# One block for the whole body, ordered on the scheduler's timeline machine, and the rest of the queries written in place

## The chip, the cores and the metric

The kernel runs on one NeuronCore of a Trainium2 chip. The metric is the device time of one execution in microseconds. Five engines work side by side, each with a queue of its own that it takes in order: TensorE (PE, with its weight loads shown apart as PEld), VectorE (DVE), ScalarE (ACT), GpSimd (POOL) and SyncE (SP), which here issues every DMA.

## What is computed

A two-layer gated cross-attention network in the manner of Flamingo, on x of 4 x 512 x 512 and a context of the same size, all float32. Four residual steps follow each other:

```python
x = x + tanh(g_xattn[0]) * wkv(w, u, layernorm(x), ctx)          # a recurrence over the 512 tokens
x = x + tanh(g_ffn[0]) * bit_ffn(layernorm(x), w1, w2, w3)       # D 512, hidden 2048, 1-bit weights
x = x + tanh(g_xattn[1]) * int8_attention(layernorm(x), ctx)     # 16 heads of 32
x = x + tanh(g_ffn[1]) * ternary_linear(rms(layernorm(x)), W)    # D 512
```

- wkv keeps a running weighted mean per channel: `p, q, o` are the numerator, the denominator and the running maximum, and the output is `(A*p + E*v) / (A*q + E)`.
- bit_ffn is `(silu(Q(x) @ B1.T) * (Q(x) @ B2.T))` quantised once more and multiplied by `B3.T`. Q rounds groups of 64 channels to 8 bits, B is the sign of the weight times its mean magnitude.
- int8_attention rounds the normalised x and wq, wp to 8 bits by rows; keys and values come from the context in full precision; scores, softmax and output projection follow.
- ternary_linear rounds the rows to 8 bits and the weights to -1, 0, 1.

## The kernel before

The four batches of 512 tokens go through the same four steps. P is 128, so a batch has NT = 4 row tiles of 128 tokens, and D has NC = 4 column blocks. Until about 90 us the first batch's recurrence, the context's keys and values and the first weights are made; then the feed-forward layer of one batch runs with other work aside of it.

**Steps and places.** Each layer is a Python generator that traces a few instructions and yields. `line` (L1222) gives a generator a place on a common scale, and `run` (L1206) always advances the one whose place is lowest. The trace order is so written by hand: feed-forward of batch b (64 steps from b to b + 16/17), the recurrence of the next batch aside of it (L1334 to L1342), the attention of the batch before (L1359), and the ternary layer of the one before that (L1371).

**The order on the engines.** The trace order isn't yet the order on the chip. The tile framework's scheduler plays the traced program on a model of the chip. When an engine of the model is free, it is given, of the traced instructions whose inputs are there and whose buffer is free, the earliest traced. The order in which this happens is the order of that engine's queue in the program; buffers are given out in that order too. The model used by default is one of two that the framework has; the other one is called the timeline machine. Two means of the kernel bind the scheduler: `behind` (L135) adds an edge without a wait that keeps one instruction after another on the same engine, and `in_turn`, `next_turn` (L147, L156) use it to keep every matmul and transpose behind the last one of the turn before. `tc.keep_in_program_order` (L193) pins the statistics of the recurrent layer.

**The recurrence** (`wkv_layer`, L562) runs on chunks of 128 channels. For each of the four chunks of a batch, DVE runs three scans over 512 tokens (L599, L629, L634) and a reciprocal in two halves (L640), POOL six products and sums (L608 to L642), ACT the exponentials (L612, L614).

**The feed-forward** (`ffn_layer`, L702) has 16 units per batch, a row tile and a quarter of the hidden size each. For a unit PE multiplies twice into a PSUM bank `ff_hp` (L733); ACT L745 takes the tanh of the first, DVE L746 reads the same bank, DVE L750 multiplies the second in; `quantised` (L671) rounds the result on DVE, ACT (L684) and POOL (L685), `parts` (L690) transposes it and splits it in two for `ff_acc` (L764). The weights `wT` are loaded again for each batch by SP (L724) into a ring of five buffers.

**The attention** (`attention_layer`, L840) has 16 units per batch, a pair of heads and half of the rows each. `scores` (L937) multiplies (`s_ps`), DVE L948 takes the maxima, ACT L950 the exponentials; `turned` transposes (`pt_ps`), ACT L970 or DVE L968 copies; `values` multiplies (`o_ps`). Before them `project` (L887) makes the queries of a group of four heads. It writes the scaled queries `q` (DVE L898), their rounded half `half[0]` (ACT L903) and the rest `half[1]` (DVE L904), and stores both halves to DRAM (SP L908), from where `fetch_queries` loads them rearranged (L913).

**Row buffers.** `row` (L856) takes a buffer of 128 x 512 float32 under the tag `at_row`, of which there are ROWS = 3. `at_q`, `at_half`, the normalised rows `at_xn` (POOL L219), the projected output `at_y` and the ternary layer's `tf_xn` all take theirs from these three. A buffer is free again when everything that reads it has ended, a DMA when it has landed.

Of the kernel before, what the change touches and what calls it, by code (L numbers as in the profile page):

```python
# [11 lines left out]
F32R = mybir.dt.float32r  # L12
# [18 lines left out]
def kernel(  # L31
# [34 lines left out]


    nc = tc.nc
    NB, T, D = x.shape
    FF = w1.shape[0]  # L70
    NT, NC, NF = T // P, D // P, FF // D
# [59 lines left out]
    def bank(name, dtype=F32):  # L131

        return psum_tile(name, "m", dtype)
# [27 lines left out]
    def matmul(*args, **kwargs):  # L161
        return in_turn(nc.tensor.matmul(*args, **kwargs))  # L162
# [677 lines left out]
    def attention_layer(b, xb, pool, tiles=range(NT)):  # L840
# [5 lines left out]
        lo, n = tiles[0] * P, len(tiles) * P  # L846
# [9 lines left out]
        def row(name, dtype=F32):  # L856
            return pool.tile([P, D], dtype, name=name, tag="at_row", bufs=ROWS)
# [29 lines left out]
        def project(g):  # L887
            qp = bank("q_ps")[:, 0:n]
            for c in range(NC):
                matmul(  # L890
                    qp,
                    lhsT=wqT[:, c, g * P : (g + 1) * P],
                    rhs=xqT[:, c, lo : lo + n],
                    start=(c == 0),
                    stop=(c == NC - 1),
                )
            q = row("at_q")[:, 0:n]
            nc.vector.scalar_tensor_tensor(  # L898
                q, qp, sq[:, g : g + 1], sxb[:, lo : lo + n], ALU.mult, ALU.mult
            )  # L900
            half = [row("at_half", F32R)[:, 0:n] for _ in range(2)]
            bias = bqc[:, g : g + 1]
            nc.scalar.activation(half[0], q, AF.Identity, bias=bias)  # L903
            nc.vector.scalar_tensor_tensor(  # L904
                half[1], q, bias, half[0].bitcast(F32), ALU.add, ALU.subtract
            )
            for i in range(2):
                nc.sync.dma_start(out=qD[b][g][i, :, lo : lo + n], in_=half[i].bitcast(F32))  # L908
# [83 lines left out]
        def collect(k):  # L992
# [14 lines left out]
            )  # L1007

        project(0)
        fetch_keys(0)  # L1010
        fetch_values(0)
        fetch_queries(0)
        yield
        project(1)
        fetch_queries(1)
        yield
# [45 lines left out]
        for k in range(len(units) + 2):  # L1062
# [29 lines left out]
            if now:  # L1092
                p, h = units[k]
                if h == 0:
                    if p + 1 < NP:
                        fetch_keys(p + 1)
                    if p % 2 == 0 and p // 2 + 2 < NC:
                        next_turn()
                        project(p // 2 + 2)
                elif p % 2 and p // 2 + 1 < NC:  # L1100
                    fetch_values(p // 2 + 1)
                if k + 2 < len(units):
                    fetch_queries(k + 2)
# [320 lines left out]
```

## Time and profile before

| | |
|---|---|
| median of 3 runs | 1096.12 us (1095.92 to 1096.5) |
| the profiled execution, its own time | 1094.21 us |
| its span, first to last instruction | 1092.4 us |
| granted TensorE clock, mean | 0.956 |
| instructions | 17928 |
| HBM read, written | 148.65 MB, 39.85 MB |

Over the span, in 40 equal slices, the busy tenths (9 is 90% or more), the granted PE clock and the share of the DMA engines:

```profile
## 2 busy tenths in 40 slices
PE   3879997998879888799997886999999999878975
...
DVE  5985548757876899896769898966687866579976
ACT  5656755567545776667877576677685777877863
POOL 3831104423333254621215545412122410100000
PEclk8889999999999999999999798999999999989998
DMA  8188845464445674645576354655574563244311
```

A slice is 27.3 us. The first three hold the start, the next eight the first batch's feed-forward with weights being made; from about slice 13 to 25 the recurrence of the next batch, attention and feed-forward run together; the last six are the last batch's attention and ternary layer without feed-forward. "Idle before" in the groups and the timeline is the time an engine stood before an instruction, and the name behind the arrow is the instruction or DMA whose end released it.

### The profile page before, as it was taken

The numbers are of one execution on the slowest core, as the hardware profiler recorded it, in microseconds if no ns is written. First come the engines' busy times: TensorE is split into PE (matmuls) and PEld (weight loads), VectorE is DVE, ScalarE is ACT, GpSimd is POOL, SyncE is SP. The second block draws the span as 40 slices with busy tenths as digits, with TensorE's granted clock in tenths as the row PEclk, the third lists the DMA queues.
The fourth block names the chain that finished last, engine by engine and source line by source line (L and its number), as shares of the span: only waits on it lengthen the run. The fifth ranks groups of instructions, "written<-read, shape, count | busy, mean of one in ns | idle before, by whom it ended". The sixth has DMA issues, their size and how long they took to land.

```text
span 1092.4 us, 17928 instructions
## 1 busy us (share of the span) xinstructions
PE 943.3 (86%) x6350; PEld 680.0 (62%) x6380; DVE 827.0 (76%) x1600; ACT 729.9 (67%) x1490; POOL 320.7 (29%) x328
## 2 busy tenths in 40 slices
PE   3879997998879888799997886999999999878975
PEld 2345564565557666677775665677776777655652
DVE  5985548757876899896769898966687866579976
ACT  5656755567545776667877576677685777877863
POOL 3831104423333254621215545412122410100000
PEclk8889999999999999999999798999999999989998
DMA  8188845464445674645576354655574563244311
GB/s 288 39 272 317 323 169 190 144 221 155 154 146 181 221 234 127 231 129 169 185 234 204 121 177 133 204 195 180 184 231 156 184 210 116 59 148 116 116 42 39
DMA packets 85674, 189.68 MB, mean 174 GB/s; under 512 B 12241, under 2 KB 36817, under 8 KB 74577
## 3 DMA queue, kind: packets, MB, share of 16 engines
q1 hardware_dynamic: 85584, 188.53, 51.7%
q8 instruction: 51, 0.84, 0.3%
q14 instruction: 39, 0.31, 0.1%
HBM read 148.65 MB, written 39.85 MB: 173 GB/s over the span
## 4 chain that ended last, share of the span: by engine, by line
PE 49%; DVE 22%; ACT 14%; POOL 5%; issue 5%; DMA 4%; SPq 1%; ACTq 0%; POOLq 0%; DVEq 0%
PE ff_hp L162 15%; PE pt_ps L165 7%; PE ff_acc L162 6%; PE o_ps L162 4%; PE v_ps L162 4%; PE s_ps L162 3%; ACT at_P L950 3%; DVE wk_q L640 3%; ACT at_PT L970 3%; DVE at_nm L948 2%; PE k_ps L162 2%; DVE wk_p L634 1%; PE qr_ps L165 1%; PE tp_ps L165 1%; ACT wk_e L612 1%
## 5 line engine op out<-in xcount | busy, mean ns | idle before, releaser
L162 PE MATMUL ff_hp<-wT,xp 128*128 128x512 f32 x1024 | 275.7, 412 | 6.6 <-DVE ff_z L746 3.7
L162 PEld LDWEIGHTS ff_hp<-wT,xp 128*128 128x128 f32 x1024 | 195.4, 196 | 54.6 <-DVE ff_z L746 5.7
L950 ACT ACTIVATE at_P<-s_ps,at_nm 128x512 f32<-128x512 f32 x256 | 175.0, 690 | 45.2 <-DVE at_nm L948 43.4
L948 DVE TENSOR_REDUCE at_nm<-s_ps 128x1 f32<-128x512 f32 x256 | 166.6, 677 | 38.4 <-PE s_ps L162 37.9
L970 ACT COPY at_PT<-pt_ps 128x512 f32<-128x512 f32 x224 | 131.2, 590 | 72.6 <-PE pt_ps L165 71.9
L685 POOL TENSOR_TENSOR ff_z<-qg_b,qg_s 128x512 f32<-128x512 bf16 x64 | 71.9, 1124 | 314.6 <-ACT qg_b L684 304.7
L165 PE MATMUL pt_ps<-ident,at_P 128*128 128x128 f32 x1024 | 155.4, 280 | 9.0 <-ACT at_PT L970 4.3
L165 PEld LDWEIGHTS pt_ps<-ident,at_P 128*128 128x128 f32 x1024 | 118.1, 142 | 47.3 <-ACT at_PT L970 10.9
L162 PE MATMUL ff_acc<-wT,hr 128*128 128x512 f32 x512 | 137.6, 409 | 5.2 <-DVE hr L697 2.6
L162 PE MATMUL s_ps<-at_kR,at_qR 128*128 128x512 f32 x256 | 103.0, 464 | 24.0 <-ACT at_P L950 17.6
L162 PEld LDWEIGHTS ff_acc<-wT,hr 128*128 128x128 f32 x512 | 92.9, 191 | 26.2 <-DVE hr L697 4.2
L162 PE MATMUL o_ps<-at_PT,at_V 128*32 128x128 f32 x2048 | 75.4, 281 | 4.7 <-ACT at_PT L970 2.8
L162 PEld LDWEIGHTS o_ps<-at_PT,at_V 128*32 128x32 f32 x2048 | 54.8, 111 | 28.6 <-issue 11.6
L746 DVE SCALAR_TENSOR_TENSOR ff_z<-ff_z,ff_hp 128x512 f32<-128x512 f32 x64 | 43.4, 679 | 37.0 <-ACT ff_z L745 36.9
L745 ACT ACTIVATE ff_z<-ff_hp,coef 128x512 f32<-128x512 f32 x64 | 44.1, 688 | 40.5 <-PE ff_hp L162 38.1
L750 DVE SCALAR_TENSOR_TENSOR ff_z<-ff_hp,coef,ff_z 128x512 f32<-128x512 f32 x64 | 47.7, 745 | 30.2 <-PE ff_hp L162 30.1
L684 ACT CAST qg_b<-qg_i 128x512 bf16<-128x512 int8 x80 | 49.3, 617 | 27.4 <-DVE qg_i L680 17.3
L162 PEld LDWEIGHTS s_ps<-at_kR,at_qR 128*128 128x128 f32 x256 | 43.3, 194 | 36.4 <-ACT at_P L950 25.2
L162 PE MATMUL v_ps<-wkvT,cT 128*128 128x512 f32 x128 | 60.5, 618 | 5.5 <-DVE wT L303 2.3
L162 PE MATMUL k_ps<-cT,wkvT 128*128 128x512 f32 x128 | 61.3, 631 | 2.3 <-ACT wk_k L584 1.0
L640 DVE RECIPROCAL wk_q<-wk_q 128x256 f32<-128x256 f32 x32 | 54.5, 1722 | 3.0 <-POOL wk_q L635 1.6
L696 ACT CAST hr<-tp_ps 128x512 fp32r<-128x512 f32 x64 | 37.6, 588 | 21.7 <-PE tp_ps L165 21.7
(180 smaller groups left out, 1669.4 us busy)
## 6 DMA issues: line engine op xcount, KB each, us to landing
wT<-wD SPq DMA_DIRECT2D x72, 1024.0 KB, 5.4
wn<-in_L_ffn_w_dram SPq DMA_DIRECT2D x18, 1024.0 KB, 6.2
at_kR<-kD SPq DMA_DIRECT2D x128, 128.0 KB, 4.0
at_qR<-qD SPq DMA_DIRECT2D x256, 64.0 KB, 2.5
wD<-wT SPq DMA_DIRECT2D x12, 1024.0 KB, 4.2
kD<-k_half SPq DMA_DIRECT2D x16, 512.0 KB, 2.8
qD<-at_half SPq DMA_DIRECT2D x32, 256.0 KB, 2.2
cn<-in_ctx_dram SPq DMA_DIRECT2D x8, 512.0 KB, 5.9
```

The lines of the kernel that those rows point to most:

```text
L162: return in_turn(nc.tensor.matmul(*args, **kwargs))
L165: return in_turn(nc.tensor.transpose(*args))
L640: nc.vector.reciprocal(half, half)
L684: nc.scalar.copy(qb, qi)
L685: nc.gpsimd.tensor_tensor(grouped(src), grouped(qb), s.unsqueeze(2).to_broadcast([P, NG, GS]), ALU.mult)
L696: nc.scalar.copy(part[:, 0, :], pt)
L745: nc.scalar.activation(z, hp, AF.Tanh, scale=coef[:, 0:1])
L746: nc.vector.scalar_tensor_tensor(z, z, 1.0, hp, ALU.add, ALU.mult)
L750: nc.vector.scalar_tensor_tensor(z, hp, coef[:, 1:2], z, ALU.mult, ALU.mult)
L948: nc.vector.tensor_reduce(nm, sp, AX.X, ALU.max, negate=True)
L950: nc.scalar.activation(lanes[k, i, t], sp, AF.Exp, bias=nm, accum_out=sums[k][:, t, i : i + 1],)
L970: made[k] = nc.scalar.copy(dst, blocks(pt))
```

## The change

Two edits. The first opens a block at the start of the body, which is closed when the body ends, so that every pool, tile and instruction of the body lies in it. The block is scheduled on the timeline machine in place of the default one. The edges of `behind` and the pin of L193 are kept. The second makes `half[1]`, the rest of the queries, no buffer of its own but the buffer of `q`, read as fp32r: L904 reads `q` and writes its result over it, and SP's second store of L908 reads it from there. A projection so takes two of the three row buffers.

```diff
     nc = tc.nc
+    ctx.enter_context(tc.block(schedule_with_timeline_sim=True))
     NB, T, D = x.shape
...
             nc.vector.scalar_tensor_tensor(
                 q, qp, sq[:, g : g + 1], sxb[:, lo : lo + n], ALU.mult, ALU.mult
             )
-            half = [row("at_half", F32R)[:, 0:n] for _ in range(2)]
+            half = [row("at_half", F32R)[:, 0:n], q.bitcast(F32R)]
             bias = bqc[:, g : g + 1]
             nc.scalar.activation(half[0], q, AF.Identity, bias=bias)
             nc.vector.scalar_tensor_tensor(
                 half[1], q, bias, half[0].bitcast(F32), ALU.add, ALU.subtract
             )
```

## The prediction

> **What bounds the kernel now.** I read the busy shares first, then the chain that ended last, then the stretches of the span, then the places where TensorE (PE) stood longest.
>
> ```profile
> PE 943.3 (86%) x6350; PEld 680.0 (62%) x6380; DVE 827.0 (76%) x1600; ACT 729.9 (67%) x1490; POOL 320.7 (29%) x328
> ...
> PE 49%; DVE 22%; ACT 14%; POOL 5%; issue 5%; DMA 4%; SPq 1%; ACTq 0%; POOLq 0%; DVEq 0%
> ```
>
> PE is the longest lane, but the chain runs through it for only 49%; VectorE (DVE) holds 22% and ScalarE (ACT) 14%. PE is idle 1092.4 - 943.3 = 149.1 us, and only that time and the boundaries of the program can move: the change takes no matmul away. The stretches say where it lies.
>
> ```profile
> 91.00:318.00 227.00, 201.59 (x908) 129.57 (x907) 150.84 (x256) 133.48 (x215) 58.38 (x60) 0.99 0.55 200
> ...
> 360.00:660.00 300.00, 260.14 (x1853) 200.49 (x1859) 257.06 (x465) 210.75 (x442) 118.37 (x117) 0.95 0.55 180
> ...
> 700.00:900.00 200.00, 192.74 (x1459) 149.69 (x1470) 146.84 (x335) 142.69 (x314) 48.28 (x48) 0.99 0.59 193
> ```
>
> After the bounds and the length come busy PE, PEld, DVE, ACT and POOL. From 700 to 900 us, where no recurrent layer runs aside, PE is idle 7.3 of 200. From 360 to 660, where the recurrent (WKV) layer of the next batch runs aside on DVE and POOL, it is idle 39.9 of 300, and DVE is busy 257.1 of 300. So where PE stands, the DVE queue is nearly full, and what counts is which of its instructions comes first. One such place:
>
> ```profile
> 458.35 0.68 ACT L745 ACTIVATE ff_z<-ff_hp,coef 128x512 f32<-128x512 f32 x1
> ...
> 459.62 2.18 POOL L635 TENSOR_TENSOR wk_q<-wk_q,wk_e 128x512 f32<-128x512 f32 x1
> ...
> 461.83 1.75 DVE L640 RECIPROCAL wk_q<-wk_q 128x256 f32<-128x256 f32 x1 [1.04 <-POOL wk_q L635]
> ...
> 463.50 0.63 DVE L746 SCALAR_TENSOR_TENSOR ff_z<-ff_z,ff_hp 128x512 f32<-128x512 f32 x1
> ...
> 464.18 2.15 PE L162 MATMUL ff_hp<-wT,xp 128*128 128x512 f32 x6 [3.67 <-DVE ff_z L746]
> ```
>
> L746 frees the PSUM bank for which the next matmuls wait. Its input is ready at 459.03, but it is queued behind L640 of the aside layer, which first waits 1.04 us for POOL and then runs 1.75; PE stands 3.67 us. The largest gap of the middle is of the same kind:
>
> ```profile
> 657.09 1.21 DVE L599 TENSOR_TENSOR_SCAN wk_o<-wc,wk_k 128x512 f32<-128x512 f32 x1
> 658.22 0.67 DVE L680 TENSOR_TENSOR qg_i<-ff_z,qg_r 128x512 int8<-128x512 f32 x1
> ...
> 658.80 0.15 DVE L1152 RECIPROCAL tf_s<-tf_s 128x1 f32<-128x1 f32 x1
> ...
> 661.05 1.11 PE L165 MATMUL qr_ps<-ident,tf_xn 128*128 128x128 f32 x4 [8.60 <-ACT tf_xn L231]
> ```
>
> A pair of reciprocals (3.37 us from 649.82) and then this scan run between the short steps on which ACT L231, and so PE, waits. From 91 to 1055 us PE has nine gaps of 2 us or more, together 32.9 us. Four follow a long DVE instruction of the aside layer: 4.13 (at 250.4), 3.67 (464.2), 2.70 (615.7), 8.60 (661.0), sum 19.1, mean 4.8. The other five sum to 13.8: 2.10, 2.21, 3.87, 2.22, 3.37.
>
> **The change, part by part.** *The other ordering machine.* It removes and adds no instruction of the computation; it may move any of the 1600 on DVE, 1490 on ACT, 328 on POOL and 621 DMA issues on SP. PE moves least: the edges of L137 to L150 hold each turn's matmuls behind the turn before, and the new block keeps them. So PE work stays at 943.3, and the price is what PE waits for. In the aside layers of batches 1 to 3, the recurrent layer has 12 chunks, each with three scans (L599, L629, L634, from 1.16 us) and two reciprocals (1.72): 60 long DVE instructions, each of which may land before something PE waits for. Today 4 of 60 do. The trace doesn't show the new order. Bounds: all nine gaps gone, -32.9; or one hit in each of the 12 chunks, 8 more at 4.8, +38.4. Between ends so far apart I go by the row it is nearest to, the stretch 360 to 660: DVE is 86% busy, so an instruction put in the wrong place finds no slack, and only 4 of 60 hits are left to be undone while 56 may be added. I take twice today's hits, +19.1, and half of the other five gaps dissolved by the reshuffle, -6.9: +12.2.
>
> The long ones also stretch each other:
>
> ```profile
> L635 POOL TENSOR_TENSOR wk_q<-wk_q,wk_e x16: 1264/1274/2192, 26.8 to 681.4; 128x512 f32<-128x512 f32 x16
> ...
> L634 DVE TENSOR_TENSOR_SCAN wk_p<-wk_e x16: 1210/1986/2293, 34.4 to 683.6; 128x512 f32<-128x512 f32 x16
> ```
>
> The columns are shortest, median and longest ns. The same shape takes 1.21 us or 2.29, so up to 1.08 us more where the two engines meet; an order that lets them meet more often pays this, and it is inside the 4.8 of a hit. The Trainium skill, page "SBUF — State Buffer", section "SBUF: two separate sides", says more: GpSimd and a DVE instruction with two SBUF inputs take one port pair in turn, and the later one is fully blocked. By that rule a meeting could cost a scan the whole 1.27 us of a POOL instruction instead of 1.08, and four new hits would cost 4 x 0.19 = 0.8 us more, an estimate of 1109 instead of the figure below; the rows show no scan that long, so the sum goes by the rows.
>
> *The block itself.* All engines enter and leave it once. No row shows such a boundary; it can't gain, as the same instructions stand before and behind. Nearest: 0.29 us of POOL idle behind its own sequencer at 0.71 us, and, as upper end, all that lies around the span, 1094.21 - 1092.4 = 1.8 us. I take the row of POOL doubled for entry and exit, +0.6.
>
> *The rest of queries over the scaled queries.* L904 still runs, 16 times at 752 ns, and writes over its own input. Each projection takes two row buffers of three instead of three. It adds a wait too: the buffer of q, before free when L904 ends, is now free when its DMA (L908) has landed, 2.2 us in the median, 4.1 at most. Queued behind that wait are the next projection's L898 on DVE, or POOL's L219 for the next normalised rows; for both, the third buffer is now free. The rows show the present wait once: ACT L903 idles 1.9 us at 361.85 for the landing of qD<-at_half, in the first layer. The tightest place is the last layer, 953 to 962 us, where no feed-forward covers: PE's gap of 3.37 at 961.64 ends with the load at_qR of the first projection, whose q, half and L908 come no earlier with the edit. So I take 0, with -1.9 (that wait gone) and +2.2 (one landing exposed) as ends. In the other three layers feed-forward matmuls (8 x 412 ns = 3.3 us a step) cover either; without them each layer would pay up to 2.2.
>
> *Sum.* +12.2 + 0.6 + 0 = +12.8 on the profiled execution, 1094.2 to 1107.0. The median of the runs is 1096.12, 1.9 above the profiled one, so I forecast 1096.1 + 12.8 = 1108.9, said as **1108**.
>
> **The rivals.** *A better order, so faster.* If the new order puts L746, L750, L948 and the short scale steps before scans and reciprocals, three of the four hits go: 3 x 4.8 = -14.3, and a quarter of the 27 gaps between 0.7 and 2 us from 91 to 700 (26.8 us), -6.7; with the block +0.6: 1096.1 - 20.4 = 1076. Two of the four hits alone: 1087. Middle: 1081. For it: 700 to 900 us shows that 3.6% idle is possible with the same feed-forward and attention, against 75.8 us idle (12.4% of 609) from 91 to 700. Against it: POOL's stretched 2.18 us at 459.62, for which L640 waited, would have to be foreseen, and DVE has little slack. It decides from the point where the hits fall below two.
>
> *SP becomes the late one.* SP issues every load and store and waits in order.
>
> ```profile
> SPq L724 <- PE ff_hp L162: 149.1, 27, 17.7
> ...
> SPq L1173 <- DVE xb L1172: 70.7, 11, 41.9
> ```
>
> L1173 stores outputs, L724 loads feed-forward weights, 1 MB each, 5.4 us to landing. If four of the weight loads come behind a store or a query store that waits (70.7 / 11 = 6.4 us each), and the five-deep ring doesn't cover them, PE waits about 4 x 6.4 = 25.7 more: with the forecast's sum 1134. For it: 16 stores and 32 query stores stand among 72 loads. Against it: today PE waits on DMAs only 4.2 us.
>
> *It does nothing on the path.* The edges hold PE, the aside work shifts within slack, and 1096.5 stays. Against it: 827 of 1092 us of DVE work may be reordered.
>
> **How the numbers follow.** Forecast (1098.5 to 1122) 0.41; SP late (above 1122) 0.17; better order (below 1094) 0.36; nothing 0.06. About 0.2% (2.2 us) is what a measurement of this kernel can tell from no change. The range leaves out one in ten on either side: 1074, a little under the better order's full price, to 1132, just short of SP's. As both signs hold most of the chance, the forecast's own range is 1099 to 1122, from half a hit more (+2.4) to a little over five (+26). Faster 0.36, same 0.06, slower 0.58.
>
> **What would show it.** Right: PE busy stays within 5 us of 943 while its idle time grows, in the stretches with the recurrent layer aside; eight or so gaps of 2 us or more end with a DVE or ACT instruction queued behind L599, L629, L634 or L640; the stretch with feed-forward and attention alone stays near 3.6% idle. Wrong: fewer such gaps and a DVE order that takes L746 before L640 (better order); PE gaps ended by wT or at_qR landings, with longer SP waits at L724 (SP late); a gap of some us at the first or last instruction (a dearer block); L898 or L219 waiting for a landing of at_half (a dearer in-place write).

## The result, and the profile after

| | before | after |
|---|---|---|
| median of the runs | 1096.02 us (1094.16 to 1096.5) | 1155.85 us (1153.67 to 1158.3) |
| ratio, 95% interval | | 1.0553 (1.0539 to 1.0567) |
| profiled execution, its span | 1092.4 us | 1151.8 us |
| granted TensorE clock, mean | 0.956 | 0.943 |
| PE idle, span less busy | 149.1 us | 194.3 us |

The change costs 60 us, five times what was forecast. Two executions further down ran far longer than the others of their kernel, at 2290 us (`block_default`) and 3972 us (`pin_dve`): they are counted in the medians and left out of the ratios. In the changed kernel every line number below the first edit is one higher (L163 is the matmul that was L162); the kernels further down add lines of their own. The busy line of the page after, and the shares of its chain of waits:

```profile
PE 957.5 (83%) x6350; PEld 689.5 (60%) x6380; DVE 831.6 (72%) x1600; ACT 730.0 (63%) x1490; POOL 320.6 (28%) x328
...
PE 48%; DVE 24%; ACT 15%; DMA 5%; issue 4%; POOL 4%; SPq 1%; ACTq 0%; DVEq 0%; POOLq 0%
```

The instructions of these engines are the same in number; ACT works as long as before, DVE 4.6 us longer. PE is idle 45.2 us longer and, with the same matmuls, busy 14.2 us longer. To see where, I cut both spans at the same instructions: the 1st, 257th, 769th and last of the 1024 `ff_hp` matmuls, which are the start of the first batch's feed-forward, of the second's, of the fourth's, and the end of it. The four stretches of the kernel after (columns as in the prediction: bounds, length, busy PE, PEld, DVE, ACT, POOL, clock, DMA share, GB/s):

```profile
0.00:109.10 109.10, 68.36 (x233) 38.04 (x233) 71.85 (x88) 67.50 (x121) 46.04 (x54) 0.84 0.68 234
109.10:364.80 255.70, 213.52 (x910) 136.06 (x910) 156.08 (x271) 128.60 (x207) 64.01 (x69) 0.92 0.47 161
364.80:790.90 426.10, 363.10 (x2523) 281.34 (x2534) 341.98 (x645) 284.50 (x595) 157.12 (x154) 0.96 0.53 175
790.90:977.40 186.50, 173.40 (x1315) 136.06 (x1324) 127.31 (x287) 125.92 (x275) 43.74 (x43) 1.00 0.54 177
```

and the second of them before:

```profile
100.20:328.60 228.40, 200.00 (x911) 130.47 (x910) 154.51 (x272) 134.12 (x215) 65.95 (x68) 0.99 0.54 192
```

Before, the four took 100.2, 228.4, 409.8 and 178.4 us. So the start loses 8.9 us, the first feed-forward 27.3, the second and third 16.3, the fourth 8.1; the rest of the span gains 1.2. Of the 27.3, half is idle time (28.4 to 42.2) and half busy time (200.0 to 213.5) at a clock of 0.92 in place of 0.99. The prediction had sized its loss by the third stretch and had nothing for the first. In the second it counted the next batch's recurrence on DVE, four of its twelve chunks, and not what ACT carries there.

How the start is lost, in the timeline of the kernel after from 21 to 37 us (start, length, engine, line, operation; idle time before it in brackets):

```profile
23.30 0.58 ACT L465 COPY cT<-ct_ps 128x512 f32<-128x512 f32 x1
...
26.24 1.90 ACT L620 ACTIVATE wk_e<-wk_e 128x2048 f32<-128x2048 f32 x1
...
28.04 0.57 ACT L465 COPY cT<-ct_ps 128x512 f32<-128x512 f32 x1
...
30.97 0.58 ACT L465 COPY cT<-ct_ps 128x512 f32<-128x512 f32 x1
...
35.70 0.58 ACT L465 COPY cT<-ct_ps 128x512 f32<-128x512 f32 x1
...
36.33 1.22 PE L163 MATMUL k_ps<-cT,wkvT 128*128 128x512 f32 x1 [6.56 <-ACT cT L465]
```

ACT does four Relus and an Exp of the recurrence between the first and the second of these four copies of the transposed context, four Relus before the third, and four Relus and an Exp before the last; PE's first `k_ps` starts at 36.33. Before, one Relu stands among the same four copies, and `k_ps` starts at 26.79:

```profile
23.52 1.05 ACT L464 COPY cT<-ct_ps 128x512 f32<-128x512 f32 x2
...
25.30 0.59 ACT L464 COPY cT<-ct_ps 128x512 f32<-128x512 f32 x1
...
26.15 0.59 ACT L464 COPY cT<-ct_ps 128x512 f32<-128x512 f32 x1 [0.27 <-PE ct_ps L165]
...
26.79 2.07 PE L162 MATMUL k_ps<-cT,wkvT 128*128 128x512 f32 x2 [0.68 <-ACT cT L464]
```

And how the fourth batch is lost, where no recurrence runs. One passage of PE after, and the same one before, each in its timeline:

```profile
819.59 2.01 PE L163 MATMUL ff_hp<-wT,xp 128*128 128x512 f32 x8
821.44 0.60 PE L166 MATMUL pt_ps<-ident,at_P 128*128 128x128 f32 x4
...
822.92 1.06 PE L163 MATMUL o_ps<-at_PT,at_V 128*32 128x128 f32 x26 [0.53 <-ACT at_PT L971]
```

```profile
767.44 0.65 PE L165 MATMUL pt_ps<-ident,at_P 128*128 128x128 f32 x4
767.85 1.87 PE L162 MATMUL ff_hp<-wT,xp 128*128 128x512 f32 x7
769.65 1.08 PE L162 MATMUL o_ps<-at_PT,at_V 128*32 128x128 f32 x32
```

Before, the attention's transposes `pt_ps` stand ahead of (nearly all) the eight `ff_hp`, which cover ACT's copy of them; after, behind, and `o_ps` waits. PE's own queue has another order.

### The profile page after: what moved, and what is told of

Its sections match the earlier page's. It is cut to its first block, busy times and chain, and to the rows that moved or that the text cites. A ratio compares the mean times of both kernels' runs of the same rounds, so it can differ in the third digit from the quotient of the medians.

```text
span 1151.8 us, 17938 instructions
## 1 busy us (share of the span) xinstructions
PE 957.5 (83%) x6350; PEld 689.5 (60%) x6380; DVE 831.6 (72%) x1600; ACT 730.0 (63%) x1490; POOL 320.6 (28%) x328
## 4 chain that ended last, share of the span: by engine, by line
PE 48%; DVE 24%; ACT 15%; DMA 5%; issue 4%; POOL 4%; SPq 1%; ACTq 0%; DVEq 0%; POOLq 0%
PE ff_hp L163 14%; PE ff_acc L163 8%; PE pt_ps L166 6%; PE o_ps L163 5%; PE v_ps L163 4%; DVE at_nm L949 3%; PE s_ps L163 3%; ACT at_PT L971 2%; DVE wk_q L641 2%; ACT at_P L951 2%; ACT wk_e L613 2%; PE tp_ps L166 1%; DVE ff_z L751 1%; PE k_ps L163 1%; DVE qg_s L223 1%
## 5 line engine op out<-in xcount | busy, mean ns | idle before, releaser
L163 PE MATMUL ff_hp<-wT,xp 128*128 128x512 f32 x1024 | 271.7, 408 | 11.8 <-DVE ff_z L747 4.9
L163 PEld LDWEIGHTS ff_hp<-wT,xp 128*128 128x128 f32 x1024 | 193.0, 193 | 61.3 <-DVE ff_z L747 6.9
L971 ACT COPY at_PT<-pt_ps 128x512 f32<-128x512 f32 x224 | 131.6, 592 | 73.2 <-PE pt_ps L166 72.5
L163 PE MATMUL ff_acc<-wT,hr 128*128 128x512 f32 x512 | 141.1, 417 | 11.6 <-DVE hr L698 9.6
L166 PEld LDWEIGHTS pt_ps<-ident,at_P 128*128 128x128 f32 x1024 | 120.7, 143 | 41.7 <-issue 11.7
L163 PEld LDWEIGHTS ff_acc<-wT,hr 128*128 128x128 f32 x512 | 95.2, 195 | 33.5 <-DVE hr L698 11.4
L163 PE MATMUL s_ps<-at_kR,at_qR 128*128 128x512 f32 x256 | 99.2, 458 | 12.1 <-ACT at_P L951 7.0
L163 PE MATMUL o_ps<-at_PT,at_V 128*32 128x128 f32 x2048 | 84.5, 283 | 23.3 <-ACT at_PT L971 20.4
L163 PEld LDWEIGHTS o_ps<-at_PT,at_V 128*32 128x32 f32 x2048 | 58.1, 112 | 49.2 <-ACT at_PT L971 28.8
L163 PE MATMUL v_ps<-wkvT,cT 128*128 128x512 f32 x128 | 68.1, 683 | 9.7 <-ACT wT L302 4.8
L751 DVE SCALAR_TENSOR_TENSOR ff_z<-ff_hp,coef,ff_z 128x512 f32<-128x512 f32 x64 | 47.6, 743 | 37.3 <-PE ff_hp L163 36.6
L746 ACT ACTIVATE ff_z<-ff_hp,coef 128x512 f32<-128x512 f32 x64 | 44.1, 688 | 41.8 <-PE ff_hp L163 40.0
L163 PE MATMUL k_ps<-cT,wkvT 128*128 128x512 f32 x128 | 61.9, 636 | 9.6 <-ACT cT L465 6.6
L747 DVE SCALAR_TENSOR_TENSOR ff_z<-ff_z,ff_hp 128x512 f32<-128x512 f32 x64 | 43.2, 675 | 34.6 <-ACT ff_z L746 34.6
L163 PEld LDWEIGHTS s_ps<-at_kR,at_qR 128*128 128x128 f32 x256 | 43.0, 196 | 21.0 <-ACT at_P L951 11.5
L697 ACT CAST hr<-tp_ps 128x512 fp32r<-128x512 f32 x64 | 37.9, 592 | 25.4 <-PE tp_ps L166 25.4
```

The source lines that it names most:

```text
L166: return in_turn(nc.tensor.transpose(*args))
L697: nc.scalar.copy(part[:, 0, :], pt)
L746: nc.scalar.activation(z, hp, AF.Tanh, scale=coef[:, 0:1])
L747: nc.vector.scalar_tensor_tensor(z, z, 1.0, hp, ALU.add, ALU.mult)
L751: nc.vector.scalar_tensor_tensor(z, hp, coef[:, 1:2], z, ALU.mult, ALU.mult)
L971: made[k] = nc.scalar.copy(dst, blocks(pt))
```

## The experiments

How far the orders differ can be read from the two programs. The pairs of instructions on a queue that stand the other way round are 3710 on DVE, 1291 on ACT, 1204 on PE, 679 on SP and 183 on POOL. Of PE's, 824 are a `pt_ps` put behind an `ff_hp`, 204 a `pt_ps` behind an `s_ps`, 172 a `wt_ps` behind `ff_acc` or `ff_hp`. Against the order in which the program is traced, the default machine's program has 6727 such pairs on DVE, 1562 on ACT and 184 on PE, the timeline machine's has 9887, 2521 and 1380: it departs further from the order written by hand.

The main tool is a transplant: every instruction of one engine is held by edges without a wait to the order that it has in the other kernel's queue. `SHIFT` is that order, as distances from the order of tracing.

```diff
     run(NB + 9)
...
+    def pinned(engine, shift):
...
+        own = [
+            i
+            for i in nc.cur_bb.bb.instructions
+            if i.engine == engine and type(i).__name__ not in skip
+        ]
...
+        queue = [own[n + d] for n, d in enumerate(shift)]
+        for ins, other in zip(queue[1:], queue):
+            tc.add_manual_dep(
+                ins,
+                other.name,
...
+    pinned(mybir.EngineType.Activation, SHIFT_ACT)
```

A queue that isn't held is put in order anew by the machine, and the traces show how far it follows. (Equal instructions can't be told apart there; by this count the whole change is 3697 pairs on DVE and 1274 on ACT.) With PE's queue held to the order of before, DVE and ACT stay near the changed kernel's order, 276 and 168 pairs from it. With DVE's held, ACT comes halfway back: 717 pairs from the changed kernel's order and 787 from before's. With ACT's held, DVE stays 968 pairs from the changed kernel's. So PE is tested nearly by itself, while a run with DVE held has moved ACT as well.

The results together: ratio to before with its interval (to the kernel before in the same series of runs, where its median was 1094.3 to 1096.0 us), median, and how many us later than before the same matmul starts in the profiled execution (first `k_ps`; `ff_hp` 1, 257, 385, 769, 1024; last `f_ps`; the heads of the columns are its times before):

| kernel | ratio (95%) | median us | 26.8 | 100.2 | 328.6 | 402.0 | 738.4 | 916.8 | 1087.5 |
|---|---|---|---|---|---|---|---|---|---|
| after | 1.0553 (1.0539 to 1.0567) | 1155.85 | 9.5 | 8.8 | 36.2 | 47.8 | 52.5 | 60.6 | 59.8 |
| pin_act | 1.0553 (1.0520 to 1.0587) | 1156.54 | 0.9 | 2.9 | 24.7 | 32.6 | 54.5 | 61.4 | 64.5 |
| pin_dve | 1.0381 (1.0351 to 1.0411) | 1137.45 | 7.9 | 7.9 | 32.6 | 37.0 | 39.7 | 47.0 | 43.0 |
| pin_both | 1.0204 (1.0176 to 1.0232) | 1117.03 | -0.9 | 0.2 | 7.6 | 9.7 | 16.1 | 23.3 | 22.9 |
| pin_pe | 1.0303 (1.0266 to 1.0340) | 1127.77 | 9.1 | 9.2 | 28.6 | 39.9 | 37.9 | 36.3 | 37.8 |
| head330 | 1.0201 (1.0164 to 1.0239) | 1115.05 | -0.8 | -0.6 | -0.1 | 6.6 | 15.4 | 23.1 | 21.0 |
| pin_all | 0.9974 (0.9958 to 0.9991) | 1091.71 | 0.0 | 0.8 | 1.4 | 3.0 | 1.2 | 0.0 | -1.4 |
| trace_pe | 1.0314 (1.0291 to 1.0338) | 1129.00 | 9.6 | 9.4 | 23.7 | 34.5 | 34.9 | 35.8 | 35.1 |
| pt_first | 1.0423 (1.0395 to 1.0450) | 1141.90 | 9.0 | 7.8 | 33.1 | 45.6 | 46.1 | 47.1 | 43.5 |
| old_with_new_pe | 1.0191 (1.0171 to 1.0211) | 1116.52 | 0.2 | 1.1 | 2.6 | 4.1 | 17.9 | 23.1 | 25.7 |
| old_with_new_act | 1.1064 (1.1045 to 1.1083) | 1211.65 | 8.3 | 13.4 | 37.1 | 47.1 | 84.1 | 112.2 | 120.3 |
| old_with_new_act_pe | 1.0989 (1.0967 to 1.1012) | 1201.95 | 8.3 | 13.5 | 45.5 | 56.1 | 76.1 | 100.3 | 109.0 |
| copies_first | 1.0510 (1.0484 to 1.0535) | 1149.06 | 0.9 | 7.0 | 29.2 | 38.7 | 45.0 | 52.6 | 50.3 |
| copies_and_pe | 1.0327 (1.0305 to 1.0350) | 1130.04 | 1.1 | 9.7 | 26.4 | 36.6 | 36.5 | 38.3 | 37.1 |

**Is it the order, and nothing else?** Three kernels: the block on the default machine; the timeline machine without the in-place write; and all five queues held to the order of before.

```diff
-    ctx.enter_context(tc.block(schedule_with_timeline_sim=True))
+    ctx.enter_context(tc.block())
```

> The changed kernel with the block on the default machine: block and in-place write kept, the timeline machine gone. Theory (it is the order): the queue orders come back to those of before but for a few places, and the time to 1096, within 3 us. Rival (the block's boundary or the in-place write costs): some of the 60 us stays; a boundary of tens of us would show as idle before the first or behind the last instruction, a dear in-place write as PE gaps ended by at_qR landings.

1.0039 (1.0021 to 1.0056), 1097.65 us: as the theory had it, with 4 us left.

```diff
-            half = [row("at_half", F32R)[:, 0:n], q.bitcast(F32R)]
+            half = [row("at_half", F32R)[:, 0:n] for _ in range(2)]
```

> The changed kernel without the in-place write: the rest of queries has its own row buffer again, the timeline machine is kept. Theory (it is the order): stays at 1156, within 5 us. Rival (the in-place write has a price that only this order exposes, three row buffers being too few or enough): 10 us or more are gone.

1.0482 (1.0452 to 1.0512), 1149.41 us: nearly all of the loss stays, and 6 us by the medians, 8 by the ratios, are gone: more than the theory's 5, less than the rival's 10.

> The changed kernel, with every instruction of all five queues held by edges without a wait to the order that the kernel before has. Block, timeline machine and in-place write are kept, so only what the machine decides besides the order (which buffer is given to which tile) can differ from before. Theory (it is the order of the queues and nothing else): 1096, within 4 us. Rival (buffers given out differently, or the block): well above 1100.

0.9974 (0.9958 to 0.9991), 1091.71 us: with block, timeline machine and in-place write all kept, the whole loss is gone. It is the order of the queues. It ends 2.8 us below before (1094.5 in the same series); the in-place write may be the reason, and comes back below.

**Whose order?** ACT first, since the trace after shows the start lost there.

> The changed kernel with only ACT's queue held to the order that it has in the kernel before; DVE, POOL, PE and SP as the timeline machine puts them. Theory A (ACT's order in the start and the first feed-forward is the main cause, since there ACT runs the recurrence's Relus and the weights' magnitudes ahead of copies that PE waits for): 30 to 45 us come back, some 1111 to 1126, first k_ps matmul near 27 us instead of 36. Theory B (DVE's order, as the prediction had it): less than 15 come back, over 1141. Theory C (PE's own turns): less than 15 come back as well.

Nothing came back: theory A falls as a statement on the sum. But the row of the table shows where. The first `k_ps` is at 27.6 us as theory A had it, and at 328.6 us 11.5 us are gained; behind it all is lost again. Why isn't shown. ACT waits 107.8 us for `pt_ps` in this kernel, against 72.5 after and 71.9 before, which would fit copies that ACT's old order has early and whose input PE's new one makes late. But with DVE's order restored as well, the next run but one, this wait is as long, 105.2 us, and the gain stays.

> The changed kernel with only DVE's queue held to the order of before, the other four as the timeline machine puts them. ACT's order alone gave nothing back (1156.5), though the first 330 us lost 25 instead of 36 us with it. Theory B (DVE's order is the main cause): 40 or more of the 62 us come back, below 1116. Theory C (PE's turns or SP's issues): 15 or less come back, above 1140. Theory D (the orders must fit each other, and an old order on one engine beside a new one on the others gains little): between, 1120 to 1150.

1137.45 us, 19 us back: theory D, between. ACT's order came halfway back with it and may have a part in this.

> The changed kernel with DVE's and ACT's queues held to the order of before, PE, POOL and SP as the timeline machine puts them. Theories B and D (DVE and ACT, the engines that PE waits for): 1096 to 1106. Theory C (PE's turns or SP's issues): above 1130.

1117.03 us, 38 us back: less than B and D have it, more than C.

> The changed kernel with only PE's queue held to the order of before. Theory C (PE's own turns, as at 434 us, where the transposes of the recurrence's output stand ahead of ready work and wait 6.37 us for DVE): 20 or more of the 62 us come back, below 1136. Theories B and D (DVE and ACT): less than 15, above 1141.

1127.77 us. Theory C's amount holds, 27 of the 60 us, though PE has the fewest moved pairs of the three. Its place doesn't: a wait of `wy_ps` of 6.4 us is in this kernel too. What is gone is the wait of `o_ps` for the copies; first the changed kernel, then this one (waited for, us in all, times, longest):

```profile
PE o_ps L163 <- ACT at_PT L971: 20.4, 25, 3.0
```

```profile
PE o_ps L165 <- ACT at_PT L973: 3.0, 3, 1.8
```

The two causes add up: ACT with DVE is worth 0.0553 - 0.0204 = 0.0349, PE 0.0553 - 0.0303 = 0.0250, together 0.0599; all five queues were worth 0.0579. So nothing is left for SP, whose queue keeps the new order in both runs. POOL can't be told apart: with ACT and DVE held, its queue is back within 37 pairs of before's (177 in the changed kernel), and no run holds it by itself.

**Which part of the span?** The chain of edges ends where before stood at 330 us, and the rest is held only behind it.

> The changed kernel with all five queues held to the order of before as far as that kernel was at 330 us, the start of the second batch's feed-forward; what follows is left to the timeline machine. The traces put 36 of the 60 us ahead of that point. If losses of the two parts simply add: 1094 + 24 = 1118 to 1124. Rival (the delays made early are slack that the later part would have lost anyway, as with ACT's order alone, where the early gain was given back): above 1140.

1115.05 us: 38 us came back, 3 more than adding has it; the rest is lost behind 330 us by itself.

**PE's order, by itself and from both sides.** `trace_pe` copies no order:

```diff
             if "ahead" in turn:
                 behind(ins, turn["ahead"])
-            turn["last"] = ins
+            turn["last"] = turn["ahead"] = ins
```

> The changed kernel with an edge from every matmul and transpose to the one traced just before it, so that PE runs in the order of the trace, where the kernel so far holds a turn only behind the last instruction of the turn before. No order is copied from the kernel before. Theory C2 (the timeline machine used the freedom that these edges leave: the attention's transposes pt_ps slid behind the feed-forward's ff_hp, and the weights' transposes wt_ps behind ff_acc): the same as with PE held to the order of before, 1123 to 1133. Rival (the order of before on PE is good for another reason than being near the trace): above 1140.

1129.0, as expected. `pt_first` binds only what is traced behind the attention's transposes:

```diff
+            if "pt" in turn:
+                behind(ins, turn["pt"])
...
-                transpose(pt[:, m * P : (m + 1) * P], w[:, m * P : (m + 1) * P], ident)
+                pts = transpose(pt[:, m * P : (m + 1) * P], w[:, m * P : (m + 1) * P], ident)
+            turn["pt"] = pts
```

> The changed kernel with edges that keep every later-traced PE instruction behind the attention's transposes pt_ps and leave all else free, wt_ps included. With all of PE held to the order of before, 22 us of delay came back, 8 of them ahead of 330 us, where no attention runs, and 14 behind. Theory C2 (pt_ps and wt_ps each cost their part): the 14 come back, 1139 to 1145. Rival (it is mostly wt_ps, and the rest follows from it): above 1148. Rival (it is mostly pt_ps): 1132 or less.

1141.9, as expected: `pt_ps` is worth 14 us. The rest of PE's share is by elimination `wt_ps`, as hardly another pair moved (no run holds it by itself): `trace_pe` has gained 12.5 us by 328.6, `pt_first` 3.1.

> The kernel before, without block and in-place write, on the default machine, with PE's queue held to the order of the changed kernel. Theory C2 (PE's order has a price by itself): 14 to 27 us slower than before, 1110 to 1123, with o_ps waiting for the copies at_PT after 360 us. Theory D (orders only have to fit each other, and the default machine fits the others around it): within 6 us of 1096.

1116.5: PE's new order costs 1.9% on the old kernel, in which DVE and ACT stay near their old order (484 and 235 pairs from it), with this wait:

```profile
PE o_ps L164 <- ACT at_PT L972: 17.3, 24, 3.2
```

**ACT's order from the other side.**

> The kernel before, on the default machine, with ACT's queue held to the order of the changed kernel. Undoing ACT's order alone gave nothing, undoing it beside DVE's gave 20 us. Theory A2 (ACT's order has a price by itself, 9 us in the first 36 us through the copies of the context behind the recurrence's Relus, and more behind it): first k_ps matmul near 36 us, and 1110 to 1122 in all. Theory D (it costs only where DVE's order is new as well): first k_ps matmul near 36 us, but most of it caught up, below 1105.

Both theories are far off: 117 us, twice the whole loss of the change. The first 328.6 us lose 37.1, as after (36.2); so for that part theory A's cause stands. Behind it, 83 us more are lost, which the changed kernel doesn't lose.

> The kernel before, on the default machine, with both ACT's and PE's queue held to the order of the changed kernel. ACT's new order alone cost 117 us there, 37 of them ahead of 330 us, as in the changed kernel, and 80 behind it, with ACT waiting 75 us for pt_ps. Theory F (ACT's new order is right for PE's new one, in which pt_ps comes late: the 80 are a misfit of the two, the 37 are ACT's own): 1096 + 36 + 12 to 24 = 1144 to 1156. Rival (ACT's order costs the 117 us wherever it stands, and DVE's new order made up for it): above 1190.

Theory F falls; 108 us stay. The same order on ACT and PE costs 60 us beside the order that the timeline machine gives DVE, and 108 beside the one that the default machine gives it (by its trace 1742 pairs from before's order and 2439 from the changed kernel's). That is as the rival has it: DVE's new order makes up for a part of ACT's. It isn't shown alone, as SP's and POOL's orders and the in-place write differ too. ACT and DVE can't be priced one by one.

**Can ACT be repaired at the source?** In `copies_first` (and with `trace_pe`'s edit, `copies_and_pe`) each Relu, Exp, Abs and Sign that is aside work goes through `aside_act`, and the copies of context and weights are remembered:

```diff
+    def aside_act(*args, **kwargs):
+        ins = nc.scalar.activation(*args, **kwargs)
+        if "last" in copies:
+            behind(ins, copies["last"])
+        return ins
```

> The changed kernel with edges on ACT alone: the recurrence's Relus and Exps and the weights' Abs and Sign are each held behind the copy out of PSUM (cT, wkvT, wT) that was traced last ahead of them. Nothing is copied from the order of before. Theory A3 (ahead of 330 us ACT's long work in front of these copies is the cause): first k_ps matmul near 27 us, 10 to 25 of the 36 us ahead of 330 come back, 1131 to 1146. Rival (only an order that fits DVE's as well helps, as with ACT held to the order of before, whose early gain was lost later): 1150 or more.

> The same edges on ACT, and PE in the order of the trace as well: the two repairs that need no other kernel's order. If their gains add: 1129 less 10 to 25, 1104 to 1119. Rival (one gives back what the other gains): 1125 or more.

1149.1, 3 us above what theory A3 allows, and 1130.0, where the rival is right: beside PE's edit, the edges on ACT bring nothing. The first `k_ps` is back at 27.7 us, and at 100.2 us all but 1.8 us of the gain is gone. The ACT timeline of `copies_first` shows a long wait between the two (L153 is the line of `aside_act`, L150 that of the copies):

```profile
61.38 0.61 ACT L153 ACTIVATE wn<-wn 128x512 f32<-128x512 f32 x1
...
70.71 0.63 ACT L153 ACTIVATE wn<-wn 128x512 f32<-128x512 f32 x1 [8.63 <-DMA wn<-in_L_ffn_w_dram]
...
73.17 0.56 ACT L150 CAST wT<-wt_ps 128x512 fp32r<-128x512 bf16 x1
```

The weights' Abs stands ahead of the next copy and waits 8.63 us for its DMA, and the copy behind it waits too. The changed kernel has 12.3 us of such waits, before 3.6. With ACT's old order (`pin_act`) they are 2.7, and at 100.2 us the kernel is 2.9 us late in place of 7.0. So it seems that one misplaced group was mended and the next one showed; no run moved these Abs alone.

**What is a hit worth?** The prediction counted four gaps behind long DVE instructions, 4.13, 3.67, 2.70 and 8.60 us. `hits_moved` has `pin_all`'s orders but for DVE instructions moved at these four places (and one on ACT), `hit_464` the second place alone, `order_of_before` is `pin_all` once more. The order of DVE's queue at the second place, in words:

```diff
-    L634 scan, L227, L640 reciprocal, L746, L640 reciprocal
+    L746, L634 scan, L227, L640 reciprocal, L640 reciprocal
```

> The changed kernel with all queues in the order of before (1091.7) but for the four places where the prediction read a hit: on DVE, L258 goes ahead of the two reciprocals at 246 us, L746 ahead of the scan at 458.7, L1036 ahead of the scan at 612, and the ternary layer's short scale steps ahead of the reciprocals at 649.8 with L231 on ACT, and the scan at 657.1 goes behind the statistics there. The gaps of before at these places are 4.13, 3.67, 2.70 and 8.60 us. Theory P (a hit is worth its gap, as the prediction took it, 4.8 on average): 12 to 17 us faster, 1075 to 1080. Rival (behind each such gap the next wait stands, and little is gained): 3 us or less, above 1088.

1.0012 (1.0000 to 1.0023), 1095.28 us: nothing gained, and some 4 us lost against the same orders without the moves (`pin_all`, 0.9974). PE in the timeline of that kernel, at the largest of the four:

```profile
652.29 0.66 PE L172 MATMUL qr_ps<-ident,tf_xn 128*128 128x128 f32 x4
656.17 1.00 PE L172 MATMUL pt_ps<-ident,at_P 128*128 128x128 f32 x4 [3.23 <-DVE at_o L1007]
...
671.43 1.11 PE L172 MATMUL pt_ps<-ident,at_P 128*128 128x128 f32 x4 [6.82 <-DVE xb L660]
```

The 8.60 us ahead of `qr_ps` are gone, and PE stands 3.23 and then 6.82 us at two later inputs from DVE. At 250 us the gap of 4.13 is gone and one of 4.65 stands behind it.

> All queues in the order of before, with one of the four moves alone: on DVE, L746 ahead of the scan at 458.7 us, so that the feed-forward's bank is free before scan, scale and reciprocal. With all four moves the traces put this place at 3.8 us gained and kept, the one at 250 us at 2.4 lost, the one at 612 at nothing, the one at 661 at 2 to 5 lost. If the places are apart: 3 to 4 us faster than the same kernel without the move, near 1088. Rival (what this one gained was caught by the others behind it as well, or was there only because the queue ran late): less than 1.5 us.

> The kernel with all queues in the order of before again, in more rounds, beside the one with a single move: what block, timeline machine and in-place write cost or bring where they can't change an order. 1091 to 1094, 0.1 to 0.4% below before (three rounds gave 0.9974). If the in-place write brings nothing by itself: 1095 to 1097.

0.9962 (0.9948 to 0.9976), 1091.01 us, against 0.9976 (0.9966 to 0.9987), 1092.26 us: 1.5 us, and the intervals overlap. So a gap of 3.67 us brought 1.5 us, and by the two intervals anything from nothing to 3.4: this doesn't rule out that it was worth its length. The kernel with the one move is the fastest of all that ran, 0.4% under before.

## Why the prediction was wrong

**The direction was right, the size was not.** It said 12.8 us for the sum and got 60. In the main the direction came right for reasons that the sum doesn't hold: of the 59.4 us by which the span grew, 14.2 are PE's slower work, put at nothing, and of the 45.2 us of idle time 11.5 lie in the start, which wasn't looked at. Between the first and the last `ff_hp` PE's idle time grew by 35.2 us, but the gaps of 2 us or more, which alone were in the sum, by 17.8 (from 8 to 14); the other half is shorter waits.

**"PE moves least: the edges of L137 to L150 hold each turn's matmuls behind the turn before, and the new block keeps them."** This step failed: it put PE's own order at nothing. The edge goes to the instruction traced last in the turn before, and leaves the others of that turn free. The timeline machine used that: 1204 pairs, 27 us with PE's order restored, 21 us on the old kernel with PE's new order. "PE work stays at 943.3" failed as well, at 957.5: nearly all of it is the first feed-forward, at a clock of 0.92 in place of 0.99. The stretch with feed-forward and attention alone, which was to stay near 3.6% idle, has 7.0% (3.0% before), by PE's order.

**The term +12.2.** It was mis-sized because of where it looked: "by the row it is nearest to, the stretch 360 to 660", with the long DVE instructions of the recurrent layer aside. That loss exists; in the kernel after, the bank that L747 frees is late behind two reciprocals:

```profile
702.03 3.35 DVE L641 RECIPROCAL wk_q<-wk_q 128x256 f32<-128x256 f32 x2
...
705.30 0.62 DVE L747 SCALAR_TENSOR_TENSOR ff_z<-ff_z,ff_hp 128x512 f32<-128x512 f32 x1
...
705.98 2.40 PE L163 MATMUL ff_hp<-wT,xp 128*128 128x512 f32 x7 [2.61 <-DVE ff_z L747]
```

In the third stretch the loss shrinks from 16.3 us to 8.5 with ACT and DVE restored. But that is 7.8 of the 60. The start and the first feed-forward lost 36 us, the start wasn't in the sum at all, and the first feed-forward only with four of the twelve chunks, some 4 us. There ACT, 61% and 59% busy before, carries the copies that PE waits for, the recurrence's Relus and Exps and the weights' sums in one queue. ACT and DVE restored together bring 38 us back, most of them there (28.6 of the 36.2). The bounds -32.9 and +38.4 came from gaps and hits on DVE alone and were too narrow by 22 us.

**The price of a hit, 4.8 us.** It didn't hold, in either direction. Four gaps of 19.1 us, shrunk or gone, gave nothing together (the one at 464 us by itself is left open): PE then waited for later inputs from the same queue. (In the example at 464 us the lines left out the scan L634, which stood ahead of L746 as well.) So the rival of a better order, priced at three hits of 4.8, fell too. In the first feed-forward, on the other hand, new waiting brought as much again in slower matmuls (below).

**The block, +0.6.** No cost shows: the time around the span is 1.8 us before and 1.9 us after (1153.67 - 1151.8), and `pin_all`, with the block, is no slower than before. No run has the block alone.

**The in-place write, 0 with -1.9 and +2.2 as ends.** Where no order can change, block and write together gain 2.6 us (0.9976, 0.9966 to 0.9987). Left to the default machine, the two cost 4.3 (1.0039), with 326 pairs of DVE instructions in another order; on the timeline machine the kernel with it stands at 1.0553 and without it at 1.0482. I priced the wait of a buffer and not the order that follows from it.

**The rival of a late SP** fell: PE's waits that a DMA ended stay small, 5.4 us in all (4.2 before), and by the sum above no share of the loss is left for SP's order.

**The rule of the Trainium skill on the shared port** ("SBUF — State Buffer", section "SBUF: two separate sides") had added 0.8 us. The 48 scans take 75.0 us after and 73.4 before, the longest 2.29 in both: neither price matters here.

What stays open: how the loss of ACT and DVE divides between them, and why the timeline machine prefers this order. No run holds DVE to its new order on the old kernel.

## What to carry to other kernels

A change of scheduler is a change of every queue at once: before pricing it, see which order is bound and which isn't, and read an edge by what it leaves free. Price it in every stage in which an engine carries short work that PE waits for beside long work that it doesn't, the start too. The length of a gap is no price: what its removal brings depends on what stands behind it in the same queue. The orders of two engines that feed each other have to be judged together.

## What the hardware showed

Waiting of PE can cost more than its length, through the granted clock. The timeline of the kernel after, and three stretches of it:

```profile
121.56 3.17 PE L163 MATMUL v_ps<-wkvT,cT 128*128 128x512 f32 x7
...
131.74 6.34 PE L163 MATMUL v_ps<-wkvT,cT 128*128 128x512 f32 x8 [2.39 <-ACT wT L302]
```

```profile
126.86:130.27 3.41, 1.58 (x17) 1.11 (x16) 2.84 (x6) 2.53 (x3) 0.00 (x0) 1.00 0.22 91
130.27:137.09 6.82, 5.35 (x7) 2.25 (x8) 0.69 (x1) 1.94 (x4) 1.04 (x1) 0.50 0.77 269
137.09:140.51 3.42, 2.83 (x18) 1.83 (x17) 0.69 (x1) 1.54 (x3) 0.00 (x0) 1.00 0.21 79
```

Eight matmuls take 6.34 us; ten us earlier seven of them took 3.17, so eight would take 8 x 3.17 / 7 = 3.62. The granted clock is 0.50 from 130.27 to 137.09 us. It fell 0.9 us into the wait of 2.39, at the end of a step of 3.41 us in which PE had been busy for 1.58. So it wasn't this wait alone: there are two more in that step, of 0.68 and 0.23 us, and together they cost these eight matmuls 2.72 us on top of the waiting. From its first record in this trace, at 17.6 us, the clock changes only at the ends of steps of 3.41 us. It fell 23 times, after steps in which PE was busy for at most 0.58 of the time (by ends that are modelled), and came back after steps of 0.88 or more; of the 271 steps behind which it stayed at 1.00, the least busy had 0.43. So how much idle time falls into one step counts, and not the length of one gap.

The first feed-forward so lost 13.8 us by waiting and, with the clock, another 13.5 by slower matmuls. In the fourth, with shorter waits, the clock stayed at 1.00 and the busy time at 173.4 us (173.0 before).

The Trainium skill, page "TensorE: Matmul & The Clock Gate", section "Part 1: The HAM clock gate (the "warmup" mystery)", says that the array falls to half its clock after an idle window of about 3.4 us and comes back after a busy one. The half and the length agree with the 0.50 and the 3.41 us here. That the window has to be idle doesn't: only 4 of the 23 falls follow a step without any work of PE.
